# Additions of returned expert rows: taking turns between the two row tiles of a pair

## The chip, the cores and the metric

The kernel runs on one core of a Trainium2 chip. The metric is the device time of one execution in microseconds (us). The engines are named as in the profile: PE is TensorE, with PEld for its weight loads; DVE is VectorE, ACT is ScalarE, POOL is GpSimd and SP is SyncE, which here only issues DMAs.

## The reference

Sixteen sequences of 256 rows with 256 features go through two residual steps. The first adds spikes, found by a running sum and a floor. The second adds a mixture of experts: a shared network, and two of eight experts for every row, weighted by gates, all divided by three.

```python
def _L1_cond_ref(x, t_emb, router_W, router_bias, w1, w3, w2, W1e, W2e):
    ...
    shared = jax.nn.silu(xf @ w1) * (xf @ w3) @ w2
    s = jax.nn.sigmoid((jnp.concatenate([xf, tf], axis=-1) @ router_W).astype(jnp.float32))
    ...
    h = jax.nn.gelu(jnp.einsum('nc,ech->enh', xf, W1e), approximate=False)
    y = jnp.einsum('enh,ehc->enc', h, W2e)
    routed = jnp.einsum('ne,enc->nc', combine, y)
    return ((shared + routed) / (N_SHARED + K)).reshape(Bb, Tt, C)
x = x + _L0_cond_ref(x, cond_1024)
x = x + _L1_cond_ref(x, cond_1024, L1_cond_router_W, ...)
```

All is in 32-bit floats, and there are 4096 rows in all.

## The kernel before

The 4096 rows are cut into 8 chunks of 512 rows, and a chunk into four row tiles of 128 rows (one row to a partition). Two neighbouring row tiles form a pair, of which there are 16. `x1ts[i]` holds chunk i after the spikes, rows on partitions, with all four tiles side by side.

The kernel has three stages. In the first, the spikes are computed chunk by chunk (`Spikes`; L370 writes the spikes of one sequence, and L378 multiplies them and adds x), the router picks two experts for each row, and each row is scattered twice into a buffer `xs` in HBM that is sorted by expert. In the second, `run_blocks` takes blocks of 128 sorted rows, runs each through its expert, and scatters the results into `ys` in HBM so that row r's two results lie at 2r and 2r + 1. In the third, `combine` fetches `ys` back, one pair at a time, and adds to each row of `x1ts` its two results times their gates.

The shared network runs beside all of this in pieces that `unit` hands out. For a chunk, `shared_hidden` makes 16 matmuls of 512 columns into `ph` (L536, three PSUM buffers), with a Silu on ACT (L546) and a product on DVE (L547) for each of four slices. `shared_out` makes 16 matmuls of 256 columns into `pa` (L563), four for each row tile; the profile records each of these matmuls, in 32-bit floats, as two, hence 32 for a chunk and eight for a row tile. They go into `p_acc`, a PSUM pool of two buffers. A DVE operation, L574, multiplies the sum by a third and adds it to the rows, which also frees the PSUM buffer. It takes two row tiles at a time, except for chunk 7 (the last), where `wide` returns 1 and each row tile has its own.

In the third stage the order on DVE is the order of the program text, under `manual_schedule(engines={DVE})`. The loop at the end alternates one or two pairs of `combine` with one piece of the shared network. The pairs go through chunks 0 to 4, then 7, then 5 and 6. Their buffers are 12 in number (`SLOTS`): four old scratch buffers, called `yc` in the profile, and eight places in the old weights' buffer, called `we`. The first 12 fetches are issued ahead by SP (L980); the other four follow when the pairs that held their buffers are done.

A row tile is added to by two operations (L996): the first, q = 0, reads `x1ts`; the second, q = 1, reads what the first wrote. Both are `scalar_tensor_tensor` of 128 x 256 elements, with the gate as a scalar for each partition. `part_done` (L589) sends finished rows out when both the shared part and the returned rows have been added. The outputs of chunks 0 to 6 are issued by POOL, two row tiles at a time; those of chunk 7 by SP, one at a time.

Of the kernel before, what the change touches and what calls it, by code (L numbers as in the profile page):

```python
# [17 lines left out]
ALU = mybir.AluOpType  # L18
# [16 lines left out]
TOPK = 2  # L35
# [3 lines left out]
def kernel(  # L39
# [34 lines left out]
    J = N // P  # L74
# [9 lines left out]
    FQ = D // NQ  # L84
# [116 lines left out]
    x1s, x1ts = {}, {}  # L201
# [348 lines left out]
    def wide(i):  # L550

        return 1 if i == NCHUNK - 1 else 2
# [31 lines left out]
    def part_done(i, j, n):  # L584
        for t in range(i * J + j, i * J + j + n):
            done[t] += 1
        if all(done[t] == 2 for t in range(i * J + j, i * J + j + n)):
            eng = nc.sync if i == NCHUNK - 1 else nc.gpsimd
            eng.dma_start(  # L589
                out=of[ts(i, N), :].rearrange("(j p) d -> p j d", p=P)[:, j : j + n],  # L590
                in_=final[i, j].rearrange("p j g f -> p j (g f)"),
            )
# [116 lines left out]
    last = ctx.enter_context(ExitStack())  # L709
# [191 lines left out]
    gates = const.tile([P, TOPK, NTT], F32)  # L901
# [68 lines left out]
    def fetch(n):  # L970

        if n < len(pairs):
            i, h = pairs[n]
            slot = n % SLOTS
            if slot < len(BACK):
                yc = tmp.tile([P, 2, TOPK, NQ, FQ], F32, tag=BACK[slot], name=f"yc_{i}_{h}")
            else:
                yc = places_w[:, slot - len(BACK)]
            rows = ys[ts(i * (J // 2) + h, 2 * P * TOPK), :]
            nc.sync.dma_start(  # L980
                out=yc.rearrange("p j q g f -> p j q (g f)"),
                in_=rows.rearrange("(j p q) d -> p j q d", p=P, q=TOPK),
            )
            ycs[n] = yc

    def combine():
        for n in range(SLOTS):
            fetch(n)
        for n, (i, h) in enumerate(pairs):
            yc = ycs.pop(n)  # L990
            for j in range(2):
                t = i * J + 2 * h + j
                last = x1ts[i][:, 2 * h + j, :, :FQ]
                for q in range(TOPK):
                    y = yc[:, j, TOPK - 1 - q]
                    nc.vector.scalar_tensor_tensor(  # L996
                        y, y, gates[:, q, t : t + 1], last, ALU.mult, ALU.add
                    )
                    last = y
            for j in range(0, 2, wide(i)):  # L1000
                final[i, 2 * h + j] = yc[:, j : j + wide(i), 0]
                part_done(i, 2 * h + j, wide(i))
            fetch(n + SLOTS)
            yield

    comb = combine()
    with tc.manual_schedule(engines={DVE}):
        unit(2)
# [46 lines left out]
```

## Time and profile before

| What | Value |
|---|---|
| Median of 3 runs | 337.07 us (336.89 to 337.3) |
| The profiled execution | 337.38 us, span 335.7 us |
| PE busy | 317.2 us, 94% of the span |
| DVE busy | 231.5 us, 69% |
| POOL busy | 165.6 us, 49% |
| ACT busy | 137.9 us, 41% |
| L996, first addition of a row tile | 32 operations, 0.48 us each, from 293.3 us on |
| L996, second addition of a row tile | 32 operations, 0.485 us each, to 328.4 us |
| Granted PE clock | 1.0 throughout |

The span is the time from the first to the last instruction in the profiled execution; the difference to its time, 1.68 us, lies around it. Recorded durations of consecutive instructions on DVE may overlap, so what they take of the engine is read from their starts. PE's matmuls are pipelined and their recorded ends are modelled.

### The profile page before, as it was taken

The numbers are of one execution on the slowest core, as the hardware profiler recorded it, in microseconds if no ns is written. First come the engines' busy times: TensorE is split into PE (matmuls) and PEld (weight loads), VectorE is DVE, ScalarE is ACT, GpSimd is POOL, SyncE is SP. The second block draws the span as 40 slices with busy tenths as digits, with TensorE's granted clock in tenths as the row PEclk, the third lists the DMA queues.
The fourth block names the chain that finished last, engine by engine and source line by source line (L and its number), as shares of the span: only waits on it lengthen the run. The fifth ranks groups of instructions, "written<-read, shape, count | busy, mean of one in ns | idle before, by whom it ended". The sixth has DMA issues, their size and how long they took to land. (4 is left out here: it accounts for less than half of the span.)

```text
span 335.7 us, 6544 instructions
## 1 busy us (share of the span) xinstructions
PE 317.2 (94%) x1674; PEld 233.9 (70%) x1674; DVE 231.5 (69%) x656; ACT 137.9 (41%) x287; POOL 165.6 (49%) x197
## 2 busy tenths in 40 slices
PE   3799998999989999999999999999999999999985
PEld 2587644547546745746699998999999998474574
DVE  4677979999999996652467655555546551299993
ACT  4547385644675372040244443444444434201100
POOL 7000274787478687662045555555555565123220
PEclk9999999999999999999999999999999999999999
DMA  6999533242222112354456665765666662499913
GB/s 174 255 217 215 146 114 98 88 136 100 79 81 99 65 64 86 109 194 102 73 109 149 155 149 142 165 140 126 156 150 151 157 146 80 164 364 408 397 70 125
DMA packets 62534, 50.34 MB, mean 150 GB/s; under 512 B 42607, under 2 KB 52864, under 8 KB 62497
## 3 DMA queue, kind: packets, MB, share of 16 engines
q1 hardware_dynamic: 42240, 26.19, 32.0%
q0 software_dynamic: 7456, 20.86, 17.0%
q10 hardware_dynamic: 12800, 2.88, 5.0%
q8 instruction: 14, 0.23, 0.3%
q14 instruction: 24, 0.19, 0.2%
HBM read 27.44 MB, written 22.84 MB: 150 GB/s over the span
## 5 line engine op out<-in xcount | busy, mean ns | idle before, releaser
L536 PE MATMUL ph<-x,w_sb 128*128 128x512 f32 (+1 forms) x288 | 119.3, 561 | 4.9 <-DVE x L378 4.2
L890 POOL DMA_INDIRECT ys<-yb,to x67 | 66.2, 988 | 67.0 <-ACT yb L889 56.4
L513 POOL DMA_INDIRECT xs<-x1t,at_i x64 | 78.8, 1232 | 38.8 <-ACT xt L291 18.7
L536 PEld LDWEIGHTS ph<-x,w_sb 128*128 128x128 f32 x288 | 54.2, 196 | 53.5 <-issue 42.0
L859 PEld LDWEIGHTS phe<-xbt,w1e 128*128 128x128 f32 x536 | 70.3, 191 | 4.7 <-ACT hbt L867 0.9
L859 PE MATMUL phe<-xbt,w1e 128*128 128x128 f32 x536 | 70.7, 275 | 0.7 <-DVE xbt L832 0.7
L881 PE MATMUL py<-we,hbt 128*128 x268 | 68.9, 380 | 0.2 <-ACT hbt L867 0.2
L827 DVE COPY w1e<-we 128x512 f32 x67 | 29.1, 435 | 45.3 <-PE phe L859 43.8
L563 PE MATMUL pa<-w_sb,hs 128*128 128x256 f32 x256 | 58.2, 381 | 1.4 <-DVE x1t L574 1.1
L563 PEld LDWEIGHTS pa<-w_sb,hs 128*128 128x128 f32 x256 | 48.0, 190 | 11.1 <-issue 2.8
L881 PEld LDWEIGHTS py<-we,hbt 128*128 128x128 f32 x268 | 45.9, 191 | 3.9 <-ACT hbt L867 0.4
L546 ACT ACTIVATE as<-ph 128x512 f32<-128x512 f32 (+1 forms) x36 | 19.9, 553 | 64.5 <-PE ph L536 51.8
L867 ACT ACTIVATE hbt<-phe 128x256 f32<-128x256 f32 x67 | 25.8, 384 | 45.6 <-PE phe L859 35.2
L547 DVE TENSOR_TENSOR hs<-as,ph 128x512 f32<-128x512 f32 (+1 forms) x36 | 22.4, 623 | 27.5 <-PE ph L536 20.8
L889 ACT COPY yb<-py 128x256 f32<-128x256 f32 x67 | 24.9, 372 | 22.7 <-PE py L881 22.2
L832 DVE STREAM_TRANSPOSE xbt<-xb 128x256 f32<-128x256 f32 x67 | 29.3, 437 | 0.0
L306 DVE TENSOR_TENSOR_SCAN tb<-keep,rates 128x1024 f32<-128x1024 f32 (+2 forms) x10 | 18.8, 1876 | 1.4 <-ACT rates L282 1.3
L497 ACT COPY x1t<-px 128x512 f32<-128x512 f32 x16 | 8.6, 592 | 25.1 <-PE px L496 25.1
L589 POOL DMA_DIRECT2D out_dram<-yc x8 | 5.8, 729 | 23.9 <-DVE yc L996 22.1
L334 ACT ACTIVATE ta<-ta,cond_t 128x256 f32<-128x256 f32 x32 | 14.1, 498 | 8.1 <-DVE ta L321 7.1
L463 POOL COPY x1t<-first 128x16 f32<-128x16 f32 x8 | 4.2, 519 | 23.1 <-DVE first L456 23.1
L574 DVE SCALAR_TENSOR_TENSOR x1t<-pa,x1t 128x512 f32<-128x512 f32 x14 | 9.6, 684 | 6.3 <-PE pa L563 6.3
(135 smaller groups left out, 268.2 us busy)
## 6 DMA issues: line engine op xcount, KB each, us to landing
xb<-xs SPq DMA_DIRECT2D x184, 33.0 KB
yc<-ys SPq DMA_DIRECT2D x8, 512.0 KB
we<-ys SPq DMA_DIRECT2D x8, 512.0 KB
xn<-in_x_dram SPq DMA_DIRECT2D x7, 512.0 KB
xb<-xs ACTq DMA_DIRECT2D x84, 33.0 KB
we<-in_L_cond_W1e_dram SPq DMA_DIRECT2D x8, 256.0 KB
we<-in_L_cond_W2e_dram SPq DMA_DIRECT2D x8, 256.0 KB
out_dram<-yc POOLq DMA_DIRECT2D x8, 256.0 KB, 4.3
```

The lines of the kernel that those rows point to most:

```text
L513: nc.gpsimd.indirect_dma_start(out=xs_w[(i * J + j) * TOPK + q][:, :], out_offset=bass.IndirectOffsetOnAxis(ap=at_i[:, q, j : j + 1], axis=0),
L536: nc.tensor.matmul(ph, lhsT=w[:, k, ts(u, P)], rhs=x1[:, k, cols], start=(k == 0), stop=(k == KD - 1),)
L546: nc.scalar.activation(act, ps[0], AF.Silu)
L547: nc.vector.tensor_tensor(ht[:, u, cols], act, ps[1], ALU.mult)
L563: nc.tensor.matmul(pa[:, q, :], lhsT=ht[:, s, ts(n * h + q, P)], rhs=w2_sb[:, s, :], start=(s == 0), stop=(s == KS - 1),)
L827: nc.vector.tensor_copy(w, we[:, bass.ds(off, KD * HE)])
L832: nc.vector.transpose(xt.rearrange("p g k r -> p g (k r)"), block[b].pop("xb")[:, :, :FQ])
L859: nc.tensor.matmul(ph[:, m, :].rearrange("p (g r) -> p g r", r=Q), lhsT=w[:, k, ts(m, P)], rhs=xt[:, :, k, :], start=(k == 0), stop=(k == ...
L867: nc.scalar.activation(ht, ph, AF.Gelu)
L881: nc.tensor.matmul(py, lhsT=ht[:, k, :], rhs=we[:, bass.ds(off + KD * HE + k * D, D)], start=(k == 0), stop=(k == KH - 1),)
L889: nc.scalar.copy(yb, py)
L890: nc.gpsimd.indirect_dma_start(out=ys_w[b][:, :], out_offset=bass.IndirectOffsetOnAxis(ap=to[:, b : b + 1], axis=0), in_=yb, in_offset=Non ...
```

## The change

The loops over the row tile j and over the place q are exchanged. Before, a row tile got both of its additions before the other tile of the pair began. After, both tiles get their first addition and then both get their second. `last` becomes a list with an entry for each tile. The operations, their operands and their number stay the same, as does all that follows in the loop.

```diff
             yc = ycs.pop(n)
-            for j in range(2):
-                t = i * J + 2 * h + j
-                last = x1ts[i][:, 2 * h + j, :, :FQ]
-                for q in range(TOPK):
+
+            last = [x1ts[i][:, 2 * h + j, :, :FQ] for j in range(2)]
+            for q in range(TOPK):
+                for j in range(2):
+                    t = i * J + 2 * h + j
                     y = yc[:, j, TOPK - 1 - q]
                     nc.vector.scalar_tensor_tensor(
-                        y, y, gates[:, q, t : t + 1], last, ALU.mult, ALU.add
+                        y, y, gates[:, q, t : t + 1], last[j], ALU.mult, ALU.add
                     )
-                    last = y
+                    last[j] = y
             for j in range(0, 2, wide(i)):
                 final[i, 2 * h + j] = yc[:, j : j + wide(i), 0]
                 part_done(i, 2 * h + j, wide(i))
```

## The prediction

> **What bounds the kernel now.** I read the page's busy table and chain first, because they disagree on who matters, then the order of instructions on TensorE and on VectorE over the last 50 us, where the changed line runs.
>
> ```profile
> PE 317.2 (94%) x1674; PEld 233.9 (70%) x1674; DVE 231.5 (69%) x656; ACT 137.9 (41%) x287; POOL 165.6 (49%) x197
> ...
> DVE 10%; PE 3%; issue 1%; DVEq 0%
> DVE yc L996 4%; DVE we L996 4%; PE ph L536 2%; DVE hs L547 1%; PE pa L563 1%; DVE x1t L574 1%; DVE we L574 0%; DVEq L996 0%; DVEq L574 0%; DVEq L547 0%
> ```
>
> TensorE is busy 94% of the span. Yet the chain that ended last runs through VectorE: the additions of L996 are 8% of the span. The chain follows back whatever was adjacent, so it doesn't prove that VectorE holds up the end. TensorE's own order decides that (columns: start us, us, engine, line, operation, count, idle before).
>
> ```profile
> 285.46 10.57 PE L536 MATMUL ph<-x,w_sb 128*128 128x512 f32 x24 [0.70 <-ACTq L954]
> 295.87 7.07 PE L563 MATMUL pa<-w_sb,hs 128*128 128x256 f32 x32
> 302.77 13.90 PE L536 MATMUL ph<-x,w_sb 128*128 128x512 f32 x32
> 316.51 8.80 PE L563 MATMUL pa<-w_sb,hs 128*128 128x256 f32 x40
> 326.45 1.99 PE L563 MATMUL pa<-w_sb,hs 128*128 128x256 f32 x8 [1.15 <-DVE x1t L574]
> 328.74 3.72 PE L563 MATMUL pa<-w_sb,hs 128*128 128x256 f32 x16 [0.30 <-DVE we L574]
> ```
>
> From 285.46 to 325.31 TensorE has no wait: the 512-wide matmuls take 13.90/32 = 0.434 us and the 256-wide ones 7.07/32 = 0.221 and 8.80/40 = 0.220 us, in both places alike. So a faster VectorE gains nothing there. Only the last 24 matmuls wait for VectorE: 1.15 us for the L574 that frees an accumulator of `p_acc` (two buffers), 0.30 us for the next one. They would need 24 x 0.220 = 5.28 us from 325.31, hence be done at 330.59; they are done at 332.46.
>
> Now VectorE, first where a pair of row tiles is added, then in the tail:
>
> ```profile
> 295.15 0.48 DVE L996 SCALAR_TENSOR_TENSOR yc<-yc,gates,x1t 128x256 f32<-128x256 f32 x1
> 295.67 0.49 DVE L996 SCALAR_TENSOR_TENSOR yc<-yc,gates 128x256 f32<-128x256 f32 x1
> 296.07 0.48 DVE L996 SCALAR_TENSOR_TENSOR yc<-yc,gates,x1t 128x256 f32<-128x256 f32 x1
> 296.58 0.48 DVE L996 SCALAR_TENSOR_TENSOR yc<-yc,gates 128x256 f32<-128x256 f32 x1
> 296.99 0.68 DVE L547 TENSOR_TENSOR hs<-as,ph 128x512 f32<-128x512 f32 x1
> ...
> 325.71 0.68 DVE L574 SCALAR_TENSOR_TENSOR x1t<-pa,x1t 128x512 f32<-128x512 f32 x1
> ...
> 328.27 0.75 DVE L574 SCALAR_TENSOR_TENSOR we<-pa,we 128x256 f32<-128x256 f32 x2
> ...
> 332.50 0.42 DVE L574 SCALAR_TENSOR_TENSOR we<-pa,we 128x256 f32<-128x256 f32 x1 [1.30 <-PE pa L563]
> ```
>
> Read the starts, not the durations. A second addition (q = 1), which reads what the one just before it wrote, starts 0.52 us after it, 0.03 past its recorded end. An addition on the other tile starts 0.40 after its predecessor, 0.08 ahead of that end. A pair takes 0.52 + 0.40 + 0.52 + 0.40 = 1.84 us.
>
> **What the Trainium skill says.** "VectorE: DVE Perf Modes", section "The DRAIN you can't avoid", says that the next operation does not start before the pipe is empty, and that the same eight copies took the same time with a semaphore after each as with one after the last. The first half fits the 0.40 us spacing; the second doesn't extend to an operation that reads its predecessor's result, where this trace shows 0.12 us more. "Perfetto Trace Analysis", section "DVE / Act Engine Instruction", explains both: the next instruction may begin prefetching when the first has finished executing, while its recorded end is the later write acknowledgement, after which the semaphore travels. That agrees with 0.08 us of overlap without a dependency and 0.03 us of gap with one.
>
> **The change part by part.** Nothing is added or removed: 64 additions of 0.48 us, 16 fetches and the output DMAs remain. The four additions of a pair turn from A0 B0 A1 B1 (A is q = 0, B is q = 1, the digit is the tile) into A0 A1 B0 B1. Each B now reads a result written two instructions earlier. Whether distance two still costs a bubble is shown elsewhere in this trace, by instructions of the same kind:
>
> ```profile
> 69.77 1.28 DVE L370 TENSOR_TENSOR x<-tb 128x512 f32<-128x512 f32 x2
> 70.98 1.28 DVE L378 SCALAR_TENSOR_TENSOR x<-x,xt 128x512 f32<-128x512 f32 x2
> ```
>
> L370 writes the spikes of sequence 0, then of sequence 1; L378 adds x to them in the same order, so each L378 reads what came two instructions before. Starts: two in 70.98 - 69.77 = 1.21 us, 0.605 each, the spacing of independent operations of this width (296.99 to 297.58 after L547, 0.59). No bubble. So each B saves 0.12 us, a pair 0.24 and takes 1.60; over 16 pairs VectorE saves 3.84 us. From both sides: the least is 0 (the bubble follows the dependency at any distance), the most 0.24 per pair, since nothing in a pair starts closer than 0.40. I take 0.24.
>
> How much reaches the end? I lay VectorE out again with 1.60 per pair, L547 and L574 at 0.60 spacing, and "ready" from TensorE's order plus 0.05. L547 at 292.71; two pairs; L547 at 296.51 (ready 296.1); one pair would bring L574 at 298.7, but its accumulator is ready only at 299.46, so VectorE waits 0.75. L574 at 303.3 (ready 303.0), L547 at 307.1 (306.3), then 309.75 (a wait of 0.45), 313.55 (313.2), 317.35 (316.6), and L574 at 320.1 (0.5 of waiting). So some 1.7 us of the 3.84 turn into waits for TensorE. Two pairs later, L574 of chunk 6's second half stands at 323.9, ended by 324.6 where it was 326.39; TensorE wants that accumulator at 325.31: the 1.15 us wait is gone. One more pair (its first addition reads this L574, 0.72 as now): L574 of chunk 7's first tile at 326.2, ended by 326.65 against 328.69 now; TensorE wants it at 327.07: the 0.30 us wait is gone too, with 0.4 us to spare. TensorE then runs unbroken to 330.59. Behind it lie the last L574 and the last output DMA, now 335.7 - 332.46 = 3.24 us, unchanged. New span 333.83: a gain of 1.87 us. If the last matmuls keep their present 3.72/16 = 0.2325 us, TensorE ends at 325.31 + 5.58 = 330.89 and the gain is 1.57. I take 1.85.
>
> The gain tolerates a smaller saving: laid out with 0.12 per pair, the two L574 end at 324.9 and 327.06, just in time; with 0.06 the gain falls to about 1.0.
>
> What is costed at nothing. **Waits**: A1 comes 0.52 us earlier within its pair, but it reads the same fetch as A0. **Fetches**: each pair starts at most 2 us earlier. The windows' DMA bytes put the SP queue at 0.65 MB by 292 and 1.84 by 296, so pair 1 (1.05 MB) is moved by about 293.3 and is wanted at 294.91 instead of 295.15. "DMA: Bandwidth & Descriptors", section "Anatomy of one DMA", gives about 2 us of fixed cost for a transfer, which would put that landing near 295; the present start of 295.15 shows no wait, so at worst 0.24 us is lost there, ahead of the 0.75 us that VectorE waits anyway. Later pairs have 2 us or more (pair 6: moved by 301.4, wanted at 305.5; the last: 318.2 against 324.6). **SP**: fetches 12 to 15 wait for the outputs of pairs 0 to 3, which leave slightly earlier; the transfers are saturated there (about 410 GB/s until 317), so they land hardly earlier and needn't. **POOL**: its 14 outputs, 0.72 us each and 1.8 us or more apart, follow VectorE; an output waited for the last addition of its pair before and does so after. **ACT**: its activations wait for TensorE, which doesn't move before 325.
>
> **Rivals.** (1) The bubble stays, because it belongs to waiting on VectorE's own semaphore, whatever the distance. Against it: the L370/L378 starts. Time: as now, 337.07. (2) TensorE hides it: if the 1.15 and 0.30 us were not VectorE's fault but modelled artefacts, TensorE would still end at 332.46; again about 337.0. Against it: the wait ends at 326.45, 0.06 after the L574 it needs. (3) Only part arrives (0.06 to 0.1 per pair, or late fetches): 336.0. (4) Slower: alternating destinations makes all four additions wait for the previous write, 0.52 each. A pair takes 2.08, VectorE gets 16 x 0.24 = 3.84 us longer, and as no wait remains ahead of the tail, L574 and the last accumulators come that much later: 340.9. It decides once a pair's mean spacing exceeds 0.46. Against it: A1 already writes another tile than the B0 in front of it, and starts 0.40 after it.
>
> **How the numbers follow.** The profiled execution took 337.38 us (335.7 of span), 0.31 above the median of 337.07 from runs of 336.89 to 337.3; I take the gain off the median: 335.2. The main case has 0.84, case (3) 0.05, cases (1) and (2) together 0.07, case (4) 0.04. A difference of 0.2% (0.67 us) is about what a measurement of this kernel tells from none; the main case and most of (3) lie beyond it. Faster 0.88, same 0.07, slower 0.05. Range: below, 337.07 - 1.87 - 0.5 of scatter and of a shorter tail, 334.7; above, past the 1.57 gain to the partial case, 336.4. The cases left out hold some 0.15.
>
> **What would show it.** In a pair, starts 0.40 apart four times over; VectorE waiting for TensorE at the L574 of chunk 5's first half, one L547 of chunk 7 and the L574 of chunk 6's first half; TensorE without a wait after 325.3 and done near 330.6; the last output 1.85 us earlier. It is wrong if B0 starts 0.52 after A1, if TensorE still waits for an accumulator, or if another queue orders itself differently.

## The result, and the profile after

The changed kernel takes 335.12 us (median of 9 runs, 334.27 to 336.31), where before takes 337.07 (9 runs, 336.01 to 338.1). The ratio is 0.994, with a 95% interval of 0.9925 to 0.9955: 2.0 us less, between 1.5 and 2.5.

The two profiled executions differ by more, 337.38 against 334.36 us. Of this, 1.03 us lies ahead of the third stage, in code that the change doesn't touch: the stage's first L536 starts at 285.46 before and at 284.43 after. So I read the third stage by itself, from that start: to the end of the span 50.24 us before (335.7 - 285.46) and 48.17 after, 2.07 less; to the start of the last L574 47.04 before (332.50 - 285.46) and 45.05 after, 1.99 less. The second of these, called **the stretch** below, is the measure for all that follows.

The page after, busy time and chain that ended last:

```profile
PE 315.9 (95%) x1674; PEld 233.6 (70%) x1674; DVE 228.4 (69%) x656; ACT 137.9 (41%) x287; POOL 164.8 (50%) x197
...
PE 14%; DVE 0%; issue 0%
PE ph L536 7%; PE pa L563 6%; DVE we L574 0%
```

VectorE is busy 3.1 us less, and the chain has passed from VectorE to TensorE. TensorE's order in the third stage after (start, us, engine, line, operation, count):

```profile
284.43 10.57 PE L536 MATMUL ph<-x,w_sb 128*128 128x512 f32 x24 [0.70 <-ACTq L954]
294.83 7.07 PE L563 MATMUL pa<-w_sb,hs 128*128 128x256 f32 x32
301.74 13.90 PE L536 MATMUL ph<-x,w_sb 128*128 128x512 f32 x32
315.47 13.98 PE L563 MATMUL pa<-w_sb,hs 128*128 128x256 f32 x64
```

The first three groups took 10.57, 7.07 and 13.90 us before as well, to the hundredth. What had been three groups of 40, 8 and 16 matmuls, with waits of 1.15 and 0.30 us between them, is one of 64: both waits are gone. VectorE's order after (the addition is L997 now):

```profile
298.48 0.69 DVE L574 SCALAR_TENSOR_TENSOR x1t<-pa,x1t 128x512 f32<-128x512 f32 x1 [0.56 <-PE pa L563]
299.09 0.87 DVE L997 SCALAR_TENSOR_TENSOR yc<-yc,gates,x1t 128x256 f32<-128x256 f32 x2
299.88 0.88 DVE L997 SCALAR_TENSOR_TENSOR yc<-yc,gates 128x256 f32<-128x256 f32 x2
300.67 0.87 DVE L997 SCALAR_TENSOR_TENSOR we<-we,gates,x1t 128x256 f32<-128x256 f32 x2
...
308.87 0.69 DVE L547 TENSOR_TENSOR hs<-as,ph 128x512 f32<-128x512 f32 x1 [0.59 <-PE ph L536]
...
319.12 0.69 DVE L574 SCALAR_TENSOR_TENSOR x1t<-pa,x1t 128x512 f32<-128x512 f32 x1 [0.45 <-PE pa L563]
...
322.89 0.68 DVE L574 SCALAR_TENSOR_TENSOR x1t<-pa,x1t 128x512 f32<-128x512 f32 x1
...
325.20 0.42 DVE L574 SCALAR_TENSOR_TENSOR we<-pa,we 128x256 f32<-128x256 f32 x1
...
329.48 0.42 DVE L574 SCALAR_TENSOR_TENSOR we<-pa,we 128x256 f32<-128x256 f32 x1 [1.30 <-PE pa L563]
```

A line with x2 is two additions that overlap: two first ones, then two second ones. From 299.09 to 300.67 a pair takes 1.58 us, where it took 1.84. The second additions now start 0.79 after the first ones, twice 0.395: no gap. VectorE has begun to wait for TensorE in three places (0.56, 0.59 and 0.45 us), where before it came late or, at the first of them, 0.1 us early.

### The profile page after: what moved, and what is told of

Read it like the earlier page. It is cut to its first block, busy times and chain, and to the rows that moved or that the text cites. A ratio compares the mean times of both kernels' runs of the same rounds, so it can differ in the third digit from the quotient of the medians.

```text
span 332.6 us, 6544 instructions
## 1 busy us (share of the span) xinstructions
PE 315.9 (95%) x1674; PEld 233.6 (70%) x1674; DVE 228.4 (69%) x656; ACT 137.9 (41%) x287; POOL 164.8 (50%) x197
## 5 line engine op out<-in xcount | busy, mean ns | idle before, releaser
L536 PE MATMUL ph<-x,w_sb 128*128 128x512 f32 (+1 forms) x288 | 118.8, 559 | 4.8 <-DVE x L378 4.1
L536 PEld LDWEIGHTS ph<-x,w_sb 128*128 128x128 f32 x288 | 53.8, 195 | 53.2 <-issue 42.0
L563 PE MATMUL pa<-w_sb,hs 128*128 128x256 f32 x256 | 57.7, 380 | 0.0
L563 PEld LDWEIGHTS pa<-w_sb,hs 128*128 128x128 f32 x256 | 48.2, 190 | 8.9 <-issue 2.8
L574 DVE SCALAR_TENSOR_TENSOR x1t<-pa,x1t 128x512 f32<-128x512 f32 x14 | 9.6, 684 | 7.3 <-PE pa L563 7.3
```

The costliest lines, as they stand in the source:

```text
L536: nc.tensor.matmul(ph, lhsT=w[:, k, ts(u, P)], rhs=x1[:, k, cols], start=(k == 0), stop=(k == KD - 1),)
L563: nc.tensor.matmul(pa[:, q, :], lhsT=ht[:, s, ts(n * h + q, P)], rhs=w2_sb[:, s, :], start=(s == 0), stop=(s == KS - 1),)
```

## The experiments

The theory: TensorE is the bound of the third stage, and the change pays only by freeing two PSUM accumulators before TensorE wants them. The main rival: VectorE's stream of additions itself sets the end. On the two chips that all but the last of these runs used, the kernel before took 344 and 342 us in the median, from 339 to 350, so the intervals of the ratios are wide. The stretch is far steadier: the changed kernel, profiled again on one of them, started its third stage 3.64 us later (288.07 instead of 284.43) and had the same stretch to the hundredth. The kernel before was not profiled on either, so the 47.04 us that all stretches are held against come from its one profile.

**Other accumulators, additions in the old order.** The decisive experiment leaves VectorE alone and takes away what makes TensorE wait.

```diff
-            pa = p_acc.tile([P, n, D], F32, tag="acc", name=f"pa_{i}_{h}")
+            if i == NCHUNK - 1:
+                pa = p_h.tile([P, n, D], F32, tag="ph", name=f"pa_{i}_{h}")
+            else:
+                pa = p_acc.tile([P, n, D], F32, tag="acc", name=f"pa_{i}_{h}")
```

> The order of the additions is that of before; only the four PSUM accumulators of chunk 7's shared output come from the pool of three that the hidden layer has done with, so TensorE needn't wait for an accumulator in the tail. Theory (TensorE is the bound, and the change only takes away its 1.45 us of waiting for two accumulators): about 335.2 us, 1.85 below before, the third stage (first L536 there to the end) 48.3 us as after the change (before 50.24). Rival (VectorE's stream of additions sets the end): 337.07 us, third stage 50.2, since VectorE does exactly what it did.

The stretch was 46.39 us (335.79 - 289.40), the third stage to the end of the span 49.6 (339.0 - 289.40), and the ratio 1.0008 (0.9974 to 1.0041). Neither side was met, and one of VectorE's waits shows what came between (three lines were added here, so L566, L577 and L999 are L563, L574 and L996 of before):

```profile
DVE yc L999 <- DMA yc<-ys: 1.1, 1, 1.1
```

In this execution a fetch arrived late, and VectorE ran 1.1 us behind its schedule of before for the rest of the stage. The pool has three buffers, so TensorE still waited 0.72 us to make the fourth sum, until VectorE had freed the first accumulator. Even so the end came 0.65 us earlier in the stretch than before, with a VectorE that was later. I repeated it with the fourth accumulator in the old pool (the edit against the run above):

```diff
-            if i == NCHUNK - 1:
+            if i == NCHUNK - 1 and h < 3:
```

> As the first run with other accumulators (order of the additions as before), but the four of chunk 7 are now all apart: three from the hidden layer's pool, the last from the old pool, so that TensorE waits for none even where a late fetch delays VectorE. Theory: from the first L536 of the third stage to the last L574 45.05 us as after the change (before 47.04), TensorE without a wait, time 1.9 us below before. Rival (VectorE's stream sets the end): 47.0 us, time of before.

TensorE's last group, then the end of VectorE's stream:

```profile
319.96 13.98 PE L566 MATMUL pa<-w_sb,hs 128*128 128x256 f32 x64
```

```profile
329.17 0.69 DVE L577 SCALAR_TENSOR_TENSOR x1t<-pa,x1t 128x512 f32<-128x512 f32 x1
...
331.72 1.08 DVE L577 SCALAR_TENSOR_TENSOR we<-pa,we 128x256 f32<-128x256 f32 x3
333.97 0.42 DVE L577 SCALAR_TENSOR_TENSOR we<-pa,we 128x256 f32<-128x256 f32 x1 [1.17 <-PE pa L566]
```

The stage begins at 288.91 here. The L577 of chunk 6's second half (L574 before) starts 40.26 us later; before it was 40.25 (325.71 - 285.46). So VectorE is as late as it ever was, with the old gaps. Yet TensorE runs its 64 matmuls in 13.98 us, exactly as after the change, and the stretch is 45.06. To the end of the span it is 48.49 us (337.4 - 288.91), where before took 50.24 and the changed kernel 48.17; the 0.3 us of difference to the latter lies behind the last L577 and was not followed up. The rival that VectorE's stream sets the end falls. The ratio is 0.997 (0.993 to 1.001), which holds the expected 0.9944 and also no change; the verdict rests on the trace.

**Both together.** The four separate accumulators are put into the changed kernel.

> The change and the four separate accumulators together. Theory (TensorE at its floor with either alone): 45.05 us from the first L536 of the third stage to the last L574, the time of the changed kernel within the noise. Rival (each takes away a wait of its own): 0.5 us or more below the changed kernel.

The stretch was 45.06 us (336.71 - 291.65), the ratio to before 0.994 (0.9911 to 0.9968). The two remedies don't add up, since they remove the same waits. This was also the attempt at a version better than both, and it isn't one.

**Half of VectorE's additions left out**, in the new order:

```diff
-            for q in range(TOPK):
+            for q in range(1, TOPK):
```

> The order after the change, with the first addition of each row tile left out (the q = 0 result of every row is not added), 32 fewer operations on VectorE, 32 x 0.40 = 12.8 us. Theory (TensorE is at its floor after the change): no gain beyond the change, 335.1 us within 0.3, third stage 48.1 to 48.2 us. Rival (VectorE still holds up part of the tail): below 334.5, third stage under 47.5.

This kernel doesn't add the q = 0 result of any row. TensorE's last group:

```profile
325.48 13.98 PE L563 MATMUL pa<-w_sb,hs 128*128 128x256 f32 x64
```

The stretch was 45.06 us (339.50 - 294.44), and TensorE's last 64 matmuls took 13.98 again. With 32 additions fewer on VectorE, by the 0.395 us from start to start an estimated 12.6 us, nothing more is won: TensorE is at its floor there. The time by itself doesn't decide this: the ratio, 0.9912 (0.988 to 0.9943), holds the expected 335.1 us (0.9942) only at its edge and the rival's 334.5 (0.9924) well inside. But the changed kernel itself came to 0.9918 on the other chip (below), and the third stage to the end of the span was 48.26 us (342.7 - 294.44), where the theory had 48.1 to 48.2 and the rival under 47.5. The verdict rests on the trace.

**The change in a part of the pairs.** The early part is n < 12, the late one n >= 12.

```diff
-            for q in range(TOPK):
-                for j in range(2):
+            both = [(q, j) for q in range(TOPK) for j in range(2)]
+            for q, j in both if n < 12 else sorted(both, key=lambda qj: qj[1]):
+                if True:
```

> Only pairs 0 to 11 take turns; pairs 12 to 15 (behind the last L547) keep the order of before. Theory: VectorE reaches the L574 of chunk 6's first half 0.3 us ahead of TensorE, the first wait of TensorE goes, and L574 of chunk 7's first tile ends at 327.36 against 327.07 wanted: 0.3 to 0.4 us of waiting stay, gain about 1.5 us, 335.6. Rival (what is saved ahead of a VectorE wait is lost): no gain, 337.07. Rival (the end follows the share of pairs changed): 12/16 of 1.95, also 1.5, so this run doesn't tell that one apart.

> Only pairs 12 to 15 take turns. Theory: L574 of chunk 6's first half at 321.2 (before 321.45), its second half's ends at 325.7 (before 326.39), so TensorE waits 0.4 us instead of 1.15 and then 0.3 us again: gain about 1.1 us, 335.95. With early-only this adds up to more than the whole change, because either part alone nearly suffices. Rival (share of pairs changed): 4/16 of 1.95, 0.5 us, 336.6. Rival (only the savings behind the last wait of VectorE count): all of it, 335.1.

TensorE's tail with the early pairs alone, then with the late ones alone:

```profile
322.51 10.65 PE L563 MATMUL pa<-w_sb,hs 128*128 128x256 f32 x48
333.46 3.72 PE L563 MATMUL pa<-w_sb,hs 128*128 128x256 f32 x16 [0.30 <-DVE we L574]
```

```profile
323.77 8.80 PE L563 MATMUL pa<-w_sb,hs 128*128 128x256 f32 x40
332.96 5.76 PE L563 MATMUL pa<-w_sb,hs 128*128 128x256 f32 x24 [0.39 <-DVE x1t L574]
```

Early alone, no first wait is recorded any more and the second stays, with 0.30 us; the stretch is 45.75 us (337.22 - 291.47), 1.29 less than before, the ratio 0.9951 (0.9921 to 0.998). Late alone, 0.39 us of the first wait stays; the stretch is 46.03 (338.76 - 292.73), 1.01 less. Together they would make 2.30, more than the 1.99 of the whole. Shares of pairs would give 0.5 to the late part, and savings behind VectorE's last wait alone would give it everything: both fall. The late part's ratio, however, was 1.0015 (0.998 to 1.0049), which leaves out the expected 0.997, so I ran that kernel again:

> Only pairs 12 to 15 take turns, once more, for its time. Theory: first L536 of the third stage to the last L574 46.0 us, time 1.0 us below before. Rival (share of pairs changed): 46.55 us, 0.5 us below before. Rival (only savings behind the last wait of VectorE count): 45.05 us, 1.9 below.

The stretch was 46.05 us (339.15 - 293.10), and the ratio 0.9965 (0.9929 to 1.0). Of the two intervals the second holds what the trace says. They hardly overlap, and why the first came out so high is not known. For the late part alone the gain is settled by the trace and not by the measured times.

**The changed kernel again**, on the chip of the run with four separate accumulators:

> The changed kernel itself, beside the others: 1.9 us below before, first L536 of the third stage to the last L574 45.05 us. If the gain was a matter of the particular runs, it will differ here.

The ratio was 0.9918 (0.9871 to 0.9964), and the stretch 45.05 us (333.12 - 288.07).

**The gap by itself**, in a kernel that computes nothing of the reference:

```diff
+        for w in (32, 128, 256, 512, 1024):
+            for d in (1, 2, 4):
+                for n in range(16):
+                    y = tiles[w, d, n % d]
+                    nc.vector.scalar_tensor_tensor(y, y, gate, src[:, :w], ALU.mult, ALU.add)
```

> A kernel by itself that computes nothing of the reference: on VectorE alone, 16 scalar_tensor_tensor operations in a row, of 32, 128, 256, 512 and 1024 columns, taking turns over 1, 2 or 4 tiles, so that each reads what was written 1, 2 or 4 operations earlier. Theory: at distance 1 the start-to-start time is the duration plus 0.03 us, at distances 2 and 4 it is 0.12 us less, whatever the width from 128 up (256 columns: 0.52, 0.40, 0.40; 512: 0.73, 0.61, 0.61). At 32 columns two operations may be too short to cover the 0.12: 0.23 at distance 1, 0.11 at 2 or 4. Rival (the saving grows with the width, as a part of the duration): at 1024 columns about 0.3 us.

The order on VectorE (one tile, two or four tiles taking turns):

```profile
4.36 4.57 DVE L85 SCALAR_TENSOR_TENSOR one<-one,gate,src 128x32 f32<-128x32 f32 x16 [3.50 <-POOL one L79]
8.84 2.68 DVE L85 SCALAR_TENSOR_TENSOR two<-two,gate,src 128x32 f32<-128x32 f32 x16
11.44 2.68 DVE L85 SCALAR_TENSOR_TENSOR four<-four,gate,src 128x32 f32<-128x32 f32 x16
...
28.52 8.29 DVE L85 SCALAR_TENSOR_TENSOR one<-one,gate,src 128x256 f32<-128x256 f32 x16
36.73 6.42 DVE L85 SCALAR_TENSOR_TENSOR two<-two,gate,src 128x256 f32<-128x256 f32 x16
43.06 6.42 DVE L85 SCALAR_TENSOR_TENSOR four<-four,gate,src 128x256 f32<-128x256 f32 x16
...
61.87 10.68 DVE L85 SCALAR_TENSOR_TENSOR two<-two,gate,src 128x512 f32<-128x512 f32 x16
83.07 21.09 DVE L85 SCALAR_TENSOR_TENSOR one<-one,gate,src 128x1024 f32<-128x1024 f32 x16
104.08 19.22 DVE L85 SCALAR_TENSOR_TENSOR two<-two,gate,src 128x1024 f32<-128x1024 f32 x16
```

Sixteen operations have 15 steps between them. Reading the predecessor's result costs (8.29 - 6.42)/15 = 0.125 us more for each step at 256 columns, (21.09 - 19.22)/15 = 0.125 at 1024, and (4.57 - 2.68)/15 = 0.126 at 32. In this one execution it is a fixed price, the same from 32 to 1024 columns. Distance two removes all of it, and distance four nothing more. The rival of a share that grows with the width falls. What the price is made of, the write itself or the signal that it is done, is not told apart by these runs.

## Why the prediction was right

**The gap.** The step that carried the prediction, that distance two costs no gap, was read off L370 and L378. It holds: a pair takes 1.58 us (1.60 forecast), and e5's kernel shows it apart from everything else.

**The layout of VectorE.** Shifted by the 1.03 us by which the profile after starts the stage earlier, it came out nearly as written: the L574 of chunk 6 at 320.15 and 323.92 (320.1 and 323.9 forecast), that of chunk 7's first tile at 326.23 (326.2). The three forecast waits of 0.75, 0.45 and 0.5 us measured 0.56, 0.59 and 0.45, 1.60 in sum where 1.7 was forecast. The difference in the first is the fetch: pair 1 began 0.21 us late after the change, at 294.07 where 293.86 would have followed without a gap. The forecast allowed up to 0.24 there and put it ahead of a wait that swallows it, which it did.

**TensorE.** Unbroken to the end, as forecast: 329.45, or 330.48 with the shift, against 330.59. The gain in the stretch is 1.99 us where I took 1.85. Most of the difference is the price of one matmul, 13.98/64 = 0.2184 us instead of 0.220, which over 64 of them makes 0.10 us. The tail behind the last L574 stayed, 3.12 us after 3.20.

**The rivals.** That the bubble stays, or that all four additions wait, is excluded by the starts. That the recorded waits were artefacts is excluded by the other accumulators. That only a part arrives, because a pair saves no more than 0.06 to 0.1 us or a fetch comes late, is excluded too: a pair saved 0.26 us, and the late fetch cost nothing.

**What was mis-sized.** In the expectations of the partial runs I counted a wait of TensorE at its recorded idle time. With early pairs alone 0.30 us are recorded, but the stretch is 0.70 longer than the floor; with late pairs 0.39 are recorded and 0.98 lost. In the kernel before, 1.15 + 0.30 = 1.45 us were recorded and 1.99 lost. The last section adds up where the rest went. The prediction itself escaped this, because it compared ends and not waits.

## What to carry to other kernels

Where VectorE runs chains of short operations, put an operation of another chain between each producer and its reader: here that removed 0.125 us for each pair of neighbours, at no cost. In this kernel the saving reached the end only through TensorE, which waited for VectorE; lay the queue of the faster engine out against the bounding engine's order, and look for the buffer that is freed late. More accumulators did the same here as a faster VectorE, and the two didn't add up.

## What the runs showed of the hardware

A break in TensorE's stream costs more than its recorded idle. These are the eight matmuls of the kernel before that stand behind the wait of 1.15 us, the first one by itself:

```profile
326.45 0.48 PE L563 MATMUL pa<-w_sb,hs 128*128 128x256 f32 x1 [1.15 <-DVE x1t L574]
326.77 1.67 PE L563 MATMUL pa<-w_sb,hs 128*128 128x256 f32 x7
```

In the unbroken group of 64, a matmul of 256 columns starts every (13.98 - 0.379)/63 = 0.216 us and is recorded as 0.379 us long (the median of L563). So the recorded idle begins only at the end of the last record, 0.163 us after the next matmul could have started. The first matmul behind the wait is recorded as longer, and the second follows it after 0.32 us, 0.104 late. A break thus costs some 0.27 us beyond its recorded idle, and the two breaks of the kernel before make the 0.54 us that its recorded waits leave open (1.99 - 1.45). Why the second matmul is late was not tested.

A short break can also stand inside a group, where the timeline shows no wait. With early pairs alone the group of 48 took 10.65 us, where an unbroken one would take 10.53 (47 x 0.216 + 0.379), and with late pairs alone the group of 24 took 5.76, where one with a break only ahead of it would take 5.45 (23 x 0.216 + 0.379 + 0.104). These 0.12 and 0.31 us, the recorded 0.30 and 0.39, and 0.27 for the recorded break make up the 0.70 and 0.98 that the two runs lost, up to 0.01 us.

In the kernel of chains, the start-to-start time at 512 columns without the gap was (10.68 - 0.75)/15 = 0.66 us (one of them is recorded as 0.75 long), where I had expected the 0.61 of L378. At 32 columns it was (11.44 - 8.84)/16 = 0.16 us, where I had expected 0.11; the gap itself was as large as at the other widths. These operations take their scalar from a tile, as L996 does, and L378 takes a constant. That this is the reason was not tested.
